# One matmul for all four groups of an involution's quarter, with its result picked out one row later

## The chip, the cores and the metric

The kernel runs on one core of one Trainium2 chip. The metric is the device time of one execution in microseconds. A core has a matrix engine (TensorE, in the profile PE for matmuls and PEld for weight loads), three engines for elementwise work (VectorE, DVE; ScalarE, ACT; GpSimd, POOL), a SyncE queue that issues most transfers (SP), and 16 DMA engines.

## The reference

Two residual layers work on x of shape 8 x 256 x 56 x 56 in float32. The change touches the first: an involution, a 7 x 7 convolution whose kernel differs from pixel to pixel and is shared by the 16 channels of a group.

```python
def _L0_conv_ref(x, w_reduce, b_reduce, w_span, b_span):   # K = 7, PAD = 3, G = 16
    ker = jnp.einsum('bchw,oc->bohw', x, w_reduce) + b_reduce[None, :, None, None]
    ker = jnp.einsum('bchw,oc->bohw', ker, w_span) + b_span[None, :, None, None]
    ker = ker.reshape(B, G, 1, K * K, H, W)
    xp = jnp.pad(x, ((0, 0), (0, 0), (PAD, PAD), (PAD, PAD)))
    patches = jnp.stack([xp[:, :, i:i + H, j:j + W] for i in range(K) for j in range(K)], axis=2)
    patches = patches.reshape(B, G, C // G, K * K, H, W)
    out = (ker * patches).sum(axis=3)
    return out.reshape(B, C, H, W)

x = x + _L0_conv_ref(_gn(x), ...)      # _gn: group norm, 32 groups
x = x + _L1_conv_ref(_gn(x), ...)      # two 3x3 ternary convolutions, batch norms, relu
```

## The kernel before, in words

The program has four stages, one after the other: the involution, the two convolutions of the second layer (`conv_phase`, matmuls at L385), and a last pass that adds everything up. The change is in the first stage.

**Tiles of the involution.** An image is cut into four quarters of 64 channels (four groups of 16 channels each, `GQ = 4`; `GP = 2` is the number of pairs of groups). The two halves of the picture's rows lie in one tile, the upper half on partitions 0 to 63 and the lower on 64 to 127. The picture is cut into small tiles of 3 x 8 pixels (`PY`, `PX`; `NP = 24`), seven across (`TX = 7`) and ten down each half (`TY = 10`; the tenth row of tiles is only one pixel high, so it has 8 pixels a tile). A small tile's outputs depend on 9 x 14 = 126 input pixels (`NQ`). So the involution of one small tile is a matmul: 126 input pixels are the contraction, the channels are the output rows, and the columns are output pixels.

**Generating the matrices.** `generate` makes, for the next quarter, the matrices `a` of 126 x (pixels) for each small tile and each group. It is cut into 14 units a quarter (`UNITS`): matmuls into a buffer `pg` of the ring `ps_p` (L629), then the bias is added on the way out, by ScalarE for some columns (L633) and by VectorE for the rest (L638), in that order. It yields after each unit. The loop takes two units in the even rows 0 to 8, one in the odd rows 1 to 7 and none in row 9 (`PER_ROW`). For the last quarter of an image `generate` also runs `reduce` for the next image (matmuls `pk`, L526, from the same ring, evacuated by ScalarE).

**Applying them.** `apply_row` does one row of small tiles of one quarter: for each of the seven tiles, each half of the picture and each pair of groups, one matmul of 32 channels by the columns of both groups of the pair, into the buffer `pa` of the ring `ps_a` (two buffers, L662). Each channel of a pair gets the result for its own group's matrix and for the other group's. `pick_out` takes what is wanted: ScalarE scales the even group's columns by 1 or 0 per partition (L674), VectorE adds the odd group's columns by 0 or 1 (L675), both into `inv` (three buffers), and GpSimd adds `inv` to x in place (L678).

**Input pixels.** They come from DRAM: `prep` normalizes a strip of x (GpSimd, `xn`, L559), transposes it (TensorE, `pt`, L567, also from `ps_p`), copies it to `stg` (ScalarE, L570) and stores it (`xtd`), three stores that `transfer` issues one a row. `load_q` brings the input pixels of a row of tiles, four rows ahead (`NQB`, L599).

**Order.** The loop runs over 32 quarters (8 images, four each) and over ten rows of tiles, 320 rows in all. In the order of the text, a row stores a part of the quarter before or loads a part of the next image (rows `X_AT`), issues one store of a strip, applies the row, prefetches, takes statistics for the norms on VectorE, picks out, generates for the next quarter, and does a step of a strip (rows `STRIP_AT`, counted over the 40 rows of an image). `pin()` holds each engine to that order. The core of it:

```python
row = apply_row(b, c, a, ty)
prefetch()
...
pick_out(b, c, ty, *row)
for _ in range(PER_ROW[ty]):
    next(gen, None)
if r in STRIP_AT:
    ...
    next(strips, None)
pin()
```

`ps_p` has three buffers of 1024 elements a partition, `ps_a` two of 512.

Of the kernel before, what the change touches and what calls it, by code (L numbers as in the profile page):

```python
# [7 lines left out]
F32 = mybir.dt.float32  # L8
F32R = mybir.dt.float32r
AF = mybir.ActivationFunctionType  # L10
ALU = mybir.AluOpType
AX = mybir.AxisListType
PSUM = bass.MemoryType.PSUM
DRAM = bass.MemoryType.DRAM

P = 128
# [10 lines left out]
CH = P // 2  # L27
NCQ = C // CH
GQ = G // NCQ
GP = GQ // 2  # L30
# [3 lines left out]
PY, PX = 3, 8  # L34
TY, TX = 10, W // PX
NP = PY * PX
# [3 lines left out]
NQ = QY * QX  # L40
# [34 lines left out]
@with_exitstack  # L75
def involution_tri_block_kernel(
    ctx: ExitStack, tc: tile.TileContext,
    x, w_red, b_red, w_line, b_tile, w1, w2, g1, b1, g2, b2, grp, ident, half, out,
):
    nc = tc.nc  # L80
    out = out.rearrange("b c h w -> b c (h w)")
# [53 lines left out]
    def image_stats(st, xt, j):  # L135
        nc.vector.bn_stats(st[:, j, :], xt[:, j * NC:(j + 1) * NC])  # L136
# [293 lines left out]


    with ExitStack() as ph1:
        ps_p = ph1.enter_context(tc.tile_pool(name="ps_p", bufs=3, space=PSUM))
        ps_a = ph1.enter_context(tc.tile_pool(name="ps_a", bufs=2, space=PSUM))

        def ps_tile(name):
# [7 lines left out]
        work = ph1.enter_context(tc.tile_pool(name="work", bufs=2))  # L444

        def load_x(b, c, j):

            if j == 0:
                xs[b, c] = xpool.tile([P, NHW], F32, tag="x", name=f"x_{b}_{c}")
            part = slice(j * NHW // 2, (j + 1) * NHW // 2)  # L450
            nc.sync.dma_start(xs[b, c][:, part], x[b, c, :, part])
# [35 lines left out]
        def fixed(shape, name, src=None):  # L487
            t_ = fix.tile(shape, F32, tag=name, name=name)
            if src is not None:
                nc.scalar.dma_start(t_, src)  # L490
            return t_

        ident_sb = fixed([P, P], "ident_sb", ident)
        half_sb = fixed([P, 2], "half_sb", half)
        wr, wrn = fixed([P, NCQ, CR], "wr"), fixed([P, NCQ, 2 * CR], "wrn")
        br, brn = fixed([P, 1], "br"), fixed([P, 1], "brn")
        for j in range(2):
# [90 lines left out]
        def transfer(n=1):  # L588
            while tasks and n:
                tasks.pop(0)()  # L590
                n -= 1
# [10 lines left out]
        def views(a):  # L602

            n = NT * GQ * NP
            return (a[:NQ, :n].rearrange("q (t f) -> q t f", t=NT),
                    a[:NQ, n:].rearrange("q (t f) -> q t f", t=NE))
# [41 lines left out]
        def apply_row(b, c, a, ty):  # L648


            ps = ps_a.tile([P, 512], F32, tag="pa", name=f"pa_{b}_{c}_{ty}")
            q = loads.pop((b, c, ty))
            whole, rest = views(a)
            if ty < TY - 1:
                av, n, t0, t1 = whole, NP, ty * TX, (TY - 1 + ty) * TX
            else:
                av, n, t0, t1 = rest, PX, 0, TX
            for k in range(TX):
                for h, t in enumerate((t0, t1)):
                    for g in range(GP):  # L660
                        o = h * CH + g * 32
                        nc.tensor.matmul(ps[o:o + 32, k * 2 * n:(k + 1) * 2 * n],  # L662
                                         q[:NQ, k, o:o + 32],
                                         av[:, t + k, g * 2 * n:(g + 1) * 2 * n],
                                         start=True, stop=True)
            return ps, n

        def pick_out(b, c, ty, ps, n):

            even, odd = (ps[:, :TX * 2 * n].rearrange("c (k h p) -> c k h p", k=TX, h=2)  # L670
                         [:, :, h] for h in range(2))
            inv = work.tile([P, TX, NP], F32, tag="inv", bufs=3, name=f"inv_{b}_{c}_{ty}")
            iv = inv[:, :, :n]
            nc.scalar.activation(iv, even, AF.Copy, scale=half_sb[:, 0:1])  # L674
            nc.vector.scalar_tensor_tensor(iv, odd, half_sb[:, 1:2], iv, ALU.mult, ALU.add)  # L675
            y, m = ty * PY, n // PX
            xv = xs[b, c][:, y * W:(y + m) * W].rearrange("p (y t x) -> p y t x", t=TX, x=PX)
            nc.gpsimd.tensor_tensor(  # L678
                xv, xv, iv.rearrange("p t (y x) -> p y t x", x=PX), ALU.add)

        queue = [(b, c, ty) for b in range(B) for c in range(NCQ) for ty in range(TY)]
        loads = {}
# [1 line left out]
        def prefetch():  # L684
            if queue:
                k = queue.pop(0)
                loads[k] = load_q(*k)

        def store_x1(b, c, h):
            nc.sync.dma_start(  # L690
                x1_d[b][c // 2][c % 2 * CH:(c % 2 + 1) * CH, h * NHW:(h + 1) * NHW],
                xs[b, c][h * CH:(h + 1) * CH])
# [3 lines left out]
        def gn2_stats(b, c, ty):  # L696

            if ty == 1:
                gst[b, c] = (small.tile([P, NCB, 6], F32, tag="gn_st2", name=f"st2_{b}_{c}"), 0)
            st, j = gst[b, c]  # L700
            while j < NCB and ((j + 1) * NC <= ty * PY * W or ty == TY):
                image_stats(st, xs[b, c], j)
                j += 1
            gst[b, c] = (st, j)
            if ty == TY:
                nc.vector.bn_aggr(mv2[:, b, c, :], st.rearrange("p n s -> p (n s)"))
# [4 lines left out]
        def pin(start=False):  # L711
            here = nc.cur_bb.bb.instructions
            fresh = []
            for i in reversed(here):
                if newest.get("all") is i:
                    break
                fresh.append(i)
            newest["all"] = here[-1]
            for i in reversed(fresh):
                if i.engine in newest and not start:  # L720
                    tc.add_manual_dep(
                        i, newest[i.engine].name,
                        mybir.DependencyInfo(mybir.DependencyClass.NoSync,
                                             mybir.DependencyReason.DATA),
                        reason="order of the text")
                newest[i.engine] = i
# [13 lines left out]
        def matrices(m):  # L740
            return (apool if m % 2 == 0 else apool1).tile(
                [P, (NT * NP + NE * PX) * GQ], F32, tag=f"a{m % 2}", name=f"a_{m}")
# [11 lines left out]
        quarters = [(b, c) for b in range(B) for c in range(NCQ)]  # L754


        X_AT = (0, 1, 4, 5, 6, 7, 8, 9)
        STRIP_AT = (23, 24, 26, 27, 29, 30, 32, 33, 35, 36, 38, 39, 2, 3, 5, 6)
        for _ in range(NQB):
            prefetch()  # L760
        pin(start=True)
        last = None
        strips = iter(())
        for m, (b, c) in enumerate(quarters):
            a = a_next
            gen = iter(())
            if m + 1 < len(quarters):
                a_next = matrices(m + 1)
                gen = generate(*quarters[m + 1], a_next)
            more = b + 1 < B  # L770
            for ty in range(TY):
                r = c * TY + ty

                if last is not None and ty in (2, 3):
                    store_x1(*last, ty - 2)
                elif more and r in X_AT:
                    load_x(b + 1, X_AT.index(r) // 2, X_AT.index(r) % 2)
                transfer()

                row = apply_row(b, c, a, ty)  # L780
                prefetch()

                if more and r >= 20:
                    if r == 20:
                        norm = params(b + 1)
                    next(norm, None)
                if ty == 1 and last is not None:
                    gn2_stats(*last, TY)
                elif ty >= 2:
                    gn2_stats(b, c, ty - 1)  # L790
                if more and 4 <= r < 20:
                    gn1_stats(b + 1, (r - 4) // NCB, (r - 4) % NCB)
                pick_out(b, c, ty, *row)
                for _ in range(PER_ROW[ty]):
                    next(gen, None)
                if r in STRIP_AT:
                    if r == STRIP_AT[0] and more:
                        strips = prep(b + 1)
                    next(strips, None)
                pin()  # L800
            for _ in gen:
                pass
            last = b, c
        gn2_stats(*last, TY)
        for h in range(2):
            store_x1(*last, h)
# [103 lines left out]
```

## Time and profile before

| what | value |
|---|---|
| time, median of 3 runs | 2447.73 us (2437.09 to 2450.58) |
| span of the profiled execution | 2443.3 us, mean granted clock 0.869 |
| TensorE busy, matmuls (PE) | 1780.2 us (73%), 30120 instructions |
| TensorE busy, weight loads (PEld) | 1670.4 us (68%), 30120 instructions |
| VectorE (DVE) | 1664.7 us (68%) |
| ScalarE (ACT) | 1125.6 us (46%) |
| GpSimd (POOL) | 286.8 us (12%) |
| L662 matmuls of apply_row | 17920, 289.8 us busy |
| L674, L675, L678 of pick_out | 320 each, 393, 368 and 518 ns on average |

Busy time is not the same as being the limit: matmuls overlap, so 17920 of them with 214 ns each take only 289.8 us together. A row of the chain of waits has a start in us, a length in us, and what the program's end hung on then. A row of the waits has us in total, times, and the longest in us. A row of the timeline has a start, a length, engine, line, operation and tiles, how many were merged (x), and in brackets the idle time before it and what ended it. "Issue" is time in which an engine waited for nothing that the profile shows.

### The profile page before, as it was taken

How to read it: one execution, taken by the hardware profiler on the slowest of the kernel's cores; microseconds unless marked ns; L12 is line 12 of the kernel's file. 1: busy time of each engine (PE TensorE's matmuls, PEld its weight loads, DVE VectorE, ACT ScalarE, POOL GpSimd, SP SyncE). 2: the span in 40 equal slices, each digit the busy share in tenths (PEclk: the TensorE clock that was granted, in tenths of full speed). 3: DMA queues.
4: the chain of work that ended last, by engine and by line, in shares of the span. 5: the costliest groups of instructions: out<-in, count | busy, mean ns of one | idle time of the engine just before them, and what ended most of it. 6: DMA issues, size and time to landing. Idle time of an engine off the chain costs nothing.

```text
span 2443.3 us, 68709 instructions
## 1 busy us (share of the span) xinstructions
PE 1780.2 (73%) x30120; PEld 1670.4 (68%) x30120; DVE 1664.7 (68%) x2554; ACT 1125.6 (46%) x2020; POOL 286.8 (12%) x427
## 2 busy tenths in 40 slices
PE   3407878788787877878767999999499999980000
PEld 2307767677676767767657999999499999980000
DVE  4566555564645556465548999999499999974444
ACT  1203434434343443434325666766456577654333
POOL 1101222222122231213210000000000000000000
PEclk8658989989898998999978999999699999995555
DMA  6627796978769597877765223322433233229998
GB/s 202 203 96 223 204 266 172 269 214 229 235 194 262 171 272 204 241 233 223 219 199 197 108 108 134 135 108 81 185 124 119 108 120 150 108 99 429 429 428 377
DMA packets 220294, 493.14 MB, mean 202 GB/s; under 512 B 38446, under 2 KB 139180, under 8 KB 211292
## 3 DMA queue, kind: packets, MB, share of 16 engines
q1 hardware_dynamic: 213680, 447.66, 55.9%
q10 hardware_dynamic: 6316, 41.09, 4.1%
q8 instruction: 237, 3.88, 0.6%
q14 instruction: 61, 0.50, 0.1%
HBM read 315.88 MB, written 172.81 MB: 200 GB/s over the span
## 4 chain that ended last, share of the span: by engine, by line
PE 65%; DMA 14%; issue 9%; DVE 7%; POOL 2%; ACT 1%; SPq 1%; ACTq 0%; POOLq 0%; DVEq 0%
PE c L385 35%; PE pg L629 15%; PE pa L662 9%; DMA y1f<-y1d 4%; DMA out_y<-x1f 3%; PE pt L567 3%; PE pk L526 3%; DVE a L638 2%; DMA q<-xtd 2%; POOL xn L559 1%; DVE x1f L848 1%; DMA x1f<-x1d 1%; DMA y1d<-y 1%; ACT a L633 1%; DMA wq<-wqd 1%
## 5 line engine op out<-in xcount | busy, mean ns | idle before, releaser
L385 PE MATMUL c<-pl,wq 128*128 128x392 f32 x4608 | 857.0, 348 | 52.1 <-ACT pl L291 32.7
L385 PEld LDWEIGHTS c<-pl,wq 128*128 128x128 f32 x4608 | 855.0, 189 | 53.8 <-ACT pl L291 33.4
L638 DVE TENSOR_TENSOR a<-pg,bt 126x756 f32<-126x756 f32 (+3 forms) x640 | 393.3, 657 | 278.0 <-ACT a L633 251.8
L629 PE MATMUL pg<-kr,wl 64*126 64x140 f32 (+1 forms) x6144 | 491.7, 308 | 62.6 <-issue 38.3
L629 PEld LDWEIGHTS pg<-kr,wl 64*126 64x126 f32 x6144 | 427.9, 209 | 87.8 <-issue 63.6
L662 PE MATMUL pa<-a,q 126*32 126x48 f32 x17920 | 289.8, 214 | 200.0 <-issue 123.7
L662 PEld LDWEIGHTS pa<-a,q 126*32 126x32 f32 x17920 | 237.4, 116 | 256.6 <-issue 202.6
L633 ACT ACTIVATE a<-pg,bt 126x126 f32<-126x126 f32 x768 | 244.2, 475 | 229.2 <-PE pg L629 228.9
L674 ACT ACTIVATE inv<-pa,half_sb 128x168 f32<-128x168 f32 x320 | 125.9, 393 | 405.6 <-PE pa L662 398.4
L678 POOL TENSOR_TENSOR x<-x,inv 128x168 f32<-128x168 f32 x320 | 165.8, 518 | 877.3 <-DVE inv L675 835.9
L675 DVE SCALAR_TENSOR_TENSOR inv<-pa,half_sb,inv 128x168 f32<-128x168 f32 x320 | 117.8, 368 | 211.6 <-ACT inv L674 211.4
L291 ACT CAST pl<-r 128x812 fp32r<-128x812 f32 x192 | 162.4, 867 | 152.3 <-DVE r L286 136.5
L348 ACT ACTIVATE dummy<-y,nc 128x1568 f32<-128x1568 f32 x128 | 205.4, 1605 | 15.6 <-DVE y L371 14.3
L292 DVE TENSOR_TENSOR pl<-r,pl 128x812 fp32r<-128x812 f32 x192 | 186.9, 1001 | 30.5 <-ACT pl L291 29.6
L136 DVE BATCH_NORM_STATS2 st<-x 128x6 f32<-128x392 f32 x256 | 138.2, 557 | 10.9 <-DMA x<-in_x 10.4
L829 ACT ACTIVATE xp<-raw,bi_bn,sc_bn 128x392 f32<-128x392 f32 (+1 forms) x128 | 84.8, 720 | 72.0 <-DVE a L286 57.1
L559 POOL TENSOR_SCALAR xn<-x,gn 128x784 f32<-128x784 f32 x64 | 108.3, 1692 | 55.9 <-DMA xtd<-xn 36.0
L819 ACT ACTIVATE xp<-raw,gn 128x392 f32<-128x392 f32 (+1 forms) x128 | 85.1, 721 | 57.0 <-DVE a L286 50.9
L567 PE MATMUL pt<-ident_sb,xn 128*112 128x128 f32 x512 | 81.6, 311 | 38.1 <-POOL xn L559 33.2
L570 ACT COPY stg<-pt 112x1024 f32<-112x1024 f32 x64 | 65.8, 1028 | 83.3 <-PE pt L567 53.2
L272 POOL MEMSET xp<- 128x116 f32 x32 | 6.3, 197 | 819.7 <-DVE a L286 819.5
L846 DVE SCALAR_TENSOR_TENSOR y1f<-y2f,sc_bn,y1f 128x3136 f32<-128x3136 f32 x16 | 55.8, 3485 | 64.8 <-DMA y2f<-y2d 64.8
(127 smaller groups left out, 1369.3 us busy)
## 6 DMA issues: line engine op xcount, KB each, us to landing
q<-xtd SPq DMA_DIRECT2D x320, 441.0 KB
xtd<-stg SPq DMA_DIRECT2D x64, 448.0 KB
raw<-x1d SPq DMA_DIRECT2D x32, 812.0 KB
raw<-y1d SPq DMA_DIRECT2D x32, 812.0 KB
x<-in_x SPq DMA_DIRECT2D x64, 392.0 KB
x1d<-x SPq DMA_DIRECT2D x64, 392.0 KB
y1d<-y SPq DMA_DIRECT2D x32, 784.0 KB
y2d<-y SPq DMA_DIRECT2D x32, 784.0 KB
```

The lines of the kernel that those rows point to most:

```text
L136: nc.vector.bn_stats(st[:, j, :], xt[:, j * NC:(j + 1) * NC])
L291: nc.scalar.copy(hi, r)
L292: nc.vector.tensor_tensor(lo, r, hi.bitcast(F32), ALU.subtract)
L348: nc.scalar.activation(dummy, y[:, to], f, bias=shift[:, to:to + 1], accum_out=stats[:, to, j, n:n + 1])
L385: nc.tensor.matmul(ps[:, to, :NM], wq[:, k, t, dx, to * P:(to + 1) * P], part[:, t, :, dx:dx + W], start=(c == 0), stop=(c == last))
L559: nc.gpsimd.tensor_scalar(xn[:, :, :, :TX].rearrange("p j r k -> p r k j"), xs[b, c][:, s * SR * W:(s + 1) * SR * W].rearrange("p (r k j) ...
L567: nc.tensor.transpose(pt[:NSP, j * P:(j + 1) * P], xn[:, j].rearrange("p r k -> p (r k)"), ident_sb)
L629: nc.tensor.matmul(dst, wl[rows, c, gp, o:o + NQ], kr[py][rows, px, :], start=True, stop=True)
L633: nc.scalar.activation(whole[:, g0 + i, p0 + j], ps[:NQ, i, j * nt:(j + 1) * nt], AF.Identity, bias=bt[:, c, g0 + i, p0 + j:p0 + j + 1])
L638: nc.vector.tensor_tensor(dst[:, g0:g0 + 2, p0:p0 + nv].rearrange("q g p t -> q g t p"), ps[:NQ, :, t0 * nv:t1 * nv].rearrange("q i (t p) ...
L662: nc.tensor.matmul(ps[o:o + 32, k * 2 * n:(k + 1) * 2 * n], q[:NQ, k, o:o + 32], av[:, t + k, g * 2 * n:(g + 1) * 2 * n], start=True, stop ...
L678: nc.gpsimd.tensor_tensor(xv, xv, iv.rearrange("p t (y x) -> p y t x", x=PX), ALU.add)
```

## The change

One matmul now does 64 channels by the columns of all four groups of a quarter, so a row of tiles has half as many. Each channel gets four results, of which one is its own group's. To pick it out there are twice as many scaled copies and fused adds as before, four a row, split between ScalarE and VectorE: three scaled copies and one fused add in even rows, two and two in odd rows, so that three or two partial sums are left, which GpSimd adds to x one by one. A row is picked out one row later, after the next row's matmuls are in the order. The buffer `pa` is twice as large, and the ring `ps_p` has two buffers in place of three. The loads of x come in every second row, a strip's steps every four rows in place of three, and the two stores of a quarter in rows 3 and 5 in place of 2 and 3.

```diff
-        ps_p = ph1.enter_context(tc.tile_pool(name="ps_p", bufs=3, space=PSUM))
+        ps_p = ph1.enter_context(tc.tile_pool(name="ps_p", bufs=2, space=PSUM))
...
-            ps = ps_a.tile([P, 512], F32, tag="pa", name=f"pa_{b}_{c}_{ty}")
+            ps = ps_a.tile([P, TX + 1, P], F32, tag="pa", name=f"pa_{b}_{c}_{ty}")
...
-                    for g in range(GP):
-                        o = h * CH + g * 32
-                        nc.tensor.matmul(ps[o:o + 32, k * 2 * n:(k + 1) * 2 * n],
-                                         q[:NQ, k, o:o + 32],
-                                         av[:, t + k, g * 2 * n:(g + 1) * 2 * n],
-                                         start=True, stop=True)
+                    nc.tensor.matmul(
+                        ps[h * CH:(h + 1) * CH, k, :GQ * n],
+                        q[:NQ, k, h * CH:(h + 1) * CH], av[:, t + k], start=True, stop=True)
...
-            inv = work.tile([P, TX, NP], F32, tag="inv", bufs=3, name=f"inv_{b}_{c}_{ty}")
-            iv = inv[:, :, :n]
-            nc.scalar.activation(iv, even, AF.Copy, scale=half_sb[:, 0:1])
-            nc.vector.scalar_tensor_tensor(iv, odd, half_sb[:, 1:2], iv, ALU.mult, ALU.add)
...
+            inv = work.tile([P, 3, TX, NP], F32, tag="inv", name=f"inv_{b}_{c}_{ty}")
...
+            iv = [inv[:, j, :, :n] for j in range(3)]
+            three = ty % 2 == 0
+            for j, g in enumerate((0, 1, 2) if three else (0, 1)):
+                nc.scalar.activation(iv[j], group(g), AF.Copy, scale=own_sb[:, g:g + 1])
+            for j, g in enumerate((3,) if three else (2, 3)):
+                nc.vector.scalar_tensor_tensor(iv[j], group(g), own_sb[:, g:g + 1], iv[j],
+                                               ALU.mult, ALU.add)
...
-            nc.gpsimd.tensor_tensor(
-                xv, xv, iv.rearrange("p t (y x) -> p y t x", x=PX), ALU.add)
+            for v in iv if three else iv[:2]:
+                nc.gpsimd.tensor_tensor(
+                    xv, xv, v.rearrange("p t (y x) -> p y t x", x=PX), ALU.add)
...
-        X_AT = (0, 1, 4, 5, 6, 7, 8, 9)
-        STRIP_AT = (23, 24, 26, 27, 29, 30, 32, 33, 35, 36, 38, 39, 2, 3, 5, 6)
+        X_AT = range(0, 16, 2)
+        STRIP_AT = (23, 24, 27, 28, 31, 32, 35, 36, 39, 0, 3, 4, 7, 8, 11, 12)
...
-                if last is not None and ty in (2, 3):
-                    store_x1(*last, ty - 2)
+                if last is not None and ty in (3, 5):
+                    store_x1(*last, (ty - 3) // 2)
...
-                row = apply_row(b, c, a, ty)
+                before, row = row, apply_row(b, c, a, ty)
...
-                pick_out(b, c, ty, *row)
+
+                if before is not None:
+                    pick_out(*before)
```

The statistics of the second norm move back by a row in the same way, and the last row is picked out after the loop.

More of the change, by code (lines that the diff above doesn't have):

```diff
@@ L77, in involution_tri_block_kernel @@
     ctx: ExitStack, tc: tile.TileContext,
-    x, w_red, b_red, w_line, b_tile, w1, w2, g1, b1, g2, b2, grp, ident, half, out,
+    x, w_red, b_red, w_line, b_tile, w1, w2, g1, b1, g2, b2, grp, ident, own, out,
 ):
@@ L493, in involution_tri_block_kernel @@
         ident_sb = fixed([P, P], "ident_sb", ident)
-        half_sb = fixed([P, 2], "half_sb", half)
+        own_sb = fixed([P, GQ], "own_sb", own)
         wr, wrn = fixed([P, NCQ, CR], "wr"), fixed([P, NCQ, 2 * CR], "wrn")
@@ L659, in apply_row, with group @@
                 for h, t in enumerate((t0, t1)):
-                    for g in range(GP):
-                        o = h * CH + g * 32
-                        nc.tensor.matmul(ps[o:o + 32, k * 2 * n:(k + 1) * 2 * n],
-                                         q[:NQ, k, o:o + 32],
-                                         av[:, t + k, g * 2 * n:(g + 1) * 2 * n],
-                                         start=True, stop=True)
-            return ps, n
-        def pick_out(b, c, ty, ps, n):
-            even, odd = (ps[:, :TX * 2 * n].rearrange("c (k h p) -> c k h p", k=TX, h=2)
-                         [:, :, h] for h in range(2))
-            inv = work.tile([P, TX, NP], F32, tag="inv", bufs=3, name=f"inv_{b}_{c}_{ty}")
-            iv = inv[:, :, :n]
-            nc.scalar.activation(iv, even, AF.Copy, scale=half_sb[:, 0:1])
-            nc.vector.scalar_tensor_tensor(iv, odd, half_sb[:, 1:2], iv, ALU.mult, ALU.add)
-            y, m = ty * PY, n // PX
+                    nc.tensor.matmul(
+                        ps[h * CH:(h + 1) * CH, k, :GQ * n],
+                        q[:NQ, k, h * CH:(h + 1) * CH], av[:, t + k], start=True, stop=True)
+            return b, c, ty, ps, n
+        def pick_out(b, c, ty, ps, n):
+            y, m = ty * PY, n // PX
+            inv = work.tile([P, 3, TX, NP], F32, tag="inv", name=f"inv_{b}_{c}_{ty}")
+            def group(g):
+                return ps[:, :TX, g * n:(g + 1) * n]
+            iv = [inv[:, j, :, :n] for j in range(3)]
[5 more added lines that the diff above has]
+                                               ALU.mult, ALU.add)
             xv = xs[b, c][:, y * W:(y + m) * W].rearrange("p (y t x) -> p y t x", t=TX, x=PX)
-            nc.gpsimd.tensor_tensor(
-                xv, xv, iv.rearrange("p t (y x) -> p y t x", x=PX), ALU.add)
+            for v in iv if three else iv[:2]:
+                nc.gpsimd.tensor_tensor(
+                    xv, xv, v.rearrange("p t (y x) -> p y t x", x=PX), ALU.add)
         queue = [(b, c, ty) for b in range(B) for c in range(NCQ) for ty in range(TY)]
@@ L761, in involution_tri_block_kernel @@
         pin(start=True)
-        last = None
+        last = row = None
         strips = iter(())
@@ L786, in involution_tri_block_kernel @@
                     next(norm, None)
-                if ty == 1 and last is not None:
+                if ty == 2 and last is not None:
                     gn2_stats(*last, TY)
-                elif ty >= 2:
-                    gn2_stats(b, c, ty - 1)
+                elif ty >= 3:
+                    gn2_stats(b, c, ty - 2)
                 if more and 4 <= r < 20:
                     gn1_stats(b + 1, (r - 4) // NCB, (r - 4) % NCB)
-                pick_out(b, c, ty, *row)
+                if before is not None:
+                    pick_out(*before)
                 for _ in range(PER_ROW[ty]):
@@ L803, in involution_tri_block_kernel @@
             last = b, c
+        pick_out(*row)
         gn2_stats(*last, TY)
@@ L875 @@
                     b_tile[px + kx, py + ky, :, :, py, px] = bs[:, :, ky, kx]
-    even = np.arange(P) // 16 % 2 == 0
     ins = {
@@ L895 @@
         "ident": np.eye(P, dtype=np.float32),
-        "half": np.stack([even, ~even], axis=1).astype(np.float32),
+        "own": np.repeat(np.tile(np.eye(GQ), (2, 1)), 16, axis=0).astype(np.float32),
     }
```

## The prediction

> **What bounds the kernel now.** I read the page's slices first (TensorE is busy in tenths 7 to 8, not 9, over the first half), then the chain of waits of the involution's row loop alone, then TensorE's own waits in it, then the timeline.
>
> The row loop runs from the first L662 matmul (183 us) to the last (1278 us): 1095 us, 320 rows, 3.42 us a row. The busy time of each engine in that stretch:
>
> ```profile
> core 0: us, PE busy (x) PEld busy (x) DVE busy (x) ACT busy (x) POOL busy (x), PEclk, DMA share, GB/s
> 183.00:1278.00 1095.00, 874.69 (x25132) 774.21 (x25130) 623.50 (x1359) 435.35 (x1176) 258.26 (x376) 0.91 0.77 223
> ```
>
> TensorE works 874.7 us of it, at a mean clock of 0.91; no other engine is near. What TensorE waits for there:
>
> ```profile
> PE pa L662 <- issue: 123.7, 70, 3.9
> PE pa L662 <- DMA q<-xtd: 58.8, 7, 52.4
> PE pg L629 <- issue: 38.3, 22, 4.6
> PE br L475 <- DVE gn L158: 12.7, 7, 2.0
> PE pa L662 <- DVE a L638: 11.9, 11, 1.4
> ```
>
> Of the 58.8 us, 52.4 is one wait before the loop. Real dependencies cost some 50 us in all; 164 us (123.7 + 38.3 + 2.3 at L567) is "issue", in 94 gaps. The timeline shows one:
>
> ```profile
> 617.37 0.62 PE L662 MATMUL pa<-a,q 126*32 126x48 f32 x37
> 620.24 0.69 PE L662 MATMUL pa<-a,q 126*32 126x48 f32 x19 [2.26 <-issue]
> ```
>
> 37 + 19 = 56 records are one row's matmuls, which wait for data only before the first: TensorE stood 2.26 us inside a row with nothing to wait for but its instructions. The DMA table names the source:
>
> ```profile
> q8 instruction: 237, 3.88, 0.6%
> ```
>
> 237 packets of 3.88 MB are 16.4 KB each; the program's 60,240 TensorE instructions (30120 loads, 30120 matmuls) at 64 B make 3.86 MB. So this queue is TensorE's instruction stream, and it shares DMA engines that are 77% busy. TensorE bounds the loop, by its stream of columns and by refills that come late.
>
> **What the skill says.** Runtime: NRT & Kernel Launch, Instruction fetch mechanics: instructions come in 16 KiB blocks of 256 over a DMA queue of the engine's own, and the cost of a boundary is mostly hidden. Size and queue agree with this trace; hidden it is not (94 gaps, 1.75 us on average). TensorEngine Tiling (Array Packing), Key Properties: tiles run their weight loads and matmuls in parallel. The trace agrees: below. TensorE: Matmul & The Clock Gate, Part 1: the clock falls to half after an idle window of about 3.4 us; the 0.91 above is such a mixture, so gaps also slow the work after them.
>
> **The change part by part.**
>
> *Wider matmuls (L662).* A row had 7 x 2 x 2 = 28 matmuls, 56 records (two passes), each 32 output channels and 48 columns; it gets 14 matmuls, 28 records, 64 channels and 96 columns. What a column costs, from the reduce matmuls and a row's matmuls:
>
> ```profile
> 551.97 3.40 PE pk L526 x32
> 576.16 0.73 PE pa L662 x56
> ```
>
> The 32 pk records are 16 of 280 and 16 of 224 columns on two row halves at once: 4032 columns in each half in 3.40 us, 0.84 ns a column. Then 48 columns take 40 ns; 56 records on four column groups at once are 14 rounds, 0.57 us, which with a tail of 0.16 us is the 0.73 us measured. So the old row already runs four matmuls side by side and is bound by its columns. The new one has two groups side by side: again 14 rounds, but of 96 columns, 81 ns: 1.13 + 0.16 + some 0.01 = 1.30 us. Plus 0.57 us on 288 full rows = +164 us, all on TensorE. The last rows of a quarter (32 columns for 16) stay near 0.6 us: their old records were issue-bound (112 in 1.28 us). Bounds: 1.15 us a row (+120) if loads overlap better than I think, 1.40 (+193) if worse.
>
> *Instructions.* 17,920 of the loop's 50,262 TensorE instructions go: 196 blocks become 126. Work per block was 874.7/196 = 4.5 us, and a late block cost 1.75 us more: a refill takes some 6 us, 9 at worst (gap of 4.6). Now a block holds (874.7 + 164 - 42)/126 = 7.9 us of work, so only the slowest refills, or blocks dense in instructions, still stall. I leave 22 of the 164 us: -142 us (bounds -100 and -160).
>
> *Clock.* At 0.91, 18% of the time was at half speed, which cost at most 0.09 x 875 = 79 us. With most gaps gone I take back half: -42 us (bounds -10 and -65).
>
> *New waits.* pick_out(r-1) now follows apply_row(r) and, on ScalarE and VectorE, the additions of row r-1's generation; the ps_a buffer of r-1 is needed by apply_row(r+1). How late that is:
>
> ```profile
> 645.62 2.03 PE L629 MATMUL pg<-kr,wl 64*126 64x126 f32 x32
> 646.81 1.76 ACT L633 ACTIVATE a<-pg,bt 126x126 f32<-126x126 f32 x6 [0.53 <-PE pg L629]
> 647.57 0.67 PEld L662 LDWEIGHTS pa<-a,q 126*32 126x32 f32 x56
> 648.11 1.53 DVE L638 TENSOR_TENSOR a<-pg,bt 126x504 f32<-126x504 f32 x2 [0.46 <-ACT a L633]
> 649.56 0.56 DVE L136 BATCH_NORM_STATS2 st<-x 128x6 f32<-128x392 f32 x1
> 650.04 0.37 DVE L675 SCALAR_TENSOR_TENSOR inv<-pa,half_sb,inv 128x168 f32<-128x168 f32 x1
> ```
>
> Two units leave TensorE at 647.57; their evacuation ends at 649.64, a statistic and the pick at 650.41: 2.84 us later. Meanwhile TensorE has one row with one unit: 1.30 + 0.97 = 2.27 us. It waits 0.5 us or so after each of the four two-unit rows of a quarter that a one-unit row follows, less where a strip's transposes (1.0 us) lie between, in two fifths of them: 1.2 us a quarter. The ps_p ring falls from three buffers to two (a ps_a tile grows from 512 to 1024 elements a partition). Strips now always transpose in rows with two units (rows 4, 8, 2, 6, 0 of a quarter; before, half of them did), so each finds the buffer of the unit before last still held: evacuated 1.5 to 2.1 us after that unit, covered by only 0.7 to 1.0 us of the next. Two strips a quarter, 1.1 us more than now. At a quarter's end row 9 has 0.6 us of work, and the next row 0 waits for the pick of row 8, 0.6 us later than for the additions it waits for now. Sum 2.9 us x 32 = 93 us; I take 82, since some fall on gaps that would be there (bounds 35 and 110). Queued behind the waiting matmuls is all TensorE work.
>
> *Evacuation.* A row has 2.5 scalings, 1.5 fused adds and 2.5 GpSimd adds for one of each. ScalarE +1.5 x (288 x 0.403 + 32 x 0.308) = +189, to 624 us; VectorE +59, to 683; GpSimd about +249, to 507. All lie beside TensorE in over 1095 us; I charge them only through the waits above. Moved x loads, stores and strips: no bytes change, and the load queue has room (it waits for TensorE itself): 0. The 1168 us outside the loop don't change.
>
> Sum: +164 - 142 - 42 + 82 = +62 us; 2447.7 + 62 = 2510 us.
>
> **The rivals.**
> *The refills win* (0.20). Waits stay at 20 because the delayed pick also takes ScalarE's waits for pa (398 us) out of the evacuation's way, the refills give 160 and the clock 55: 164 - 160 - 55 + 20 = -31, 2417 us. For it: the 164 us of "issue" are the largest idle item. Against it: VectorE at 683 us with fewer buffers behind a denser TensorE.
> *A wash* (0.10). Refills -155, clock -50, waits 45: +4, 2452 us.
> *The 64-wide groups don't overlap* (0.04). 14 rounds become 28: 28 x 81 = 2.27 + 0.16 us a row, +1.70 x 288 = +490, less 160 for refills and 65 for clock: 2713 us. Against it: four 32-wide groups overlap now.
> *DMA becomes the bound.* At a share of 0.77 it could do the loop in 843 us; no reason for it.
>
> **Numbers.** Forecast 2510 us (0.66 for slower by this mechanism, 0.70 with the serial case), faster 0.20, same 0.10. The range reaches down to the first rival, 2415, and up to where pa at 1.40 us (+29), refills at -100 (+42) and waits at 110 (+28) are mostly together: 2595.
>
> **What would show it.** Right: pa row at about 1.3 us on the chain; "issue" below 50 us in the loop; mean clock there about 0.95; new TensorE waits at pa and pt for VectorE and ScalarE of 80 to 150 us in all. Wrong: a pa row under 1.0 us, "issue" still above 100 us, or pa and pt waits no more than now.

## The result, and the profile after

The changed kernel takes 2566.3 us (median), 1.051 times the time of before (95% interval 1.0468 to 1.0551; the quotient of the two medians, 1.049, lies within it). The forecast was 2510 us, slower, in a range of 2415 to 2595: right in direction and range, about half the size. All of the difference lies in the row loop, which now runs from 183 to 1399 us, 1216 us in place of 1095.

The busy time of each engine in that stretch (the same view as before):

```profile
core 0: us, PE busy (x) PEld busy (x) DVE busy (x) ACT busy (x) POOL busy (x), PEclk, DMA share, GB/s
183.00:1399.00 1216.00, 1013.34 (x16168) 899.58 (x16164) 663.87 (x1517) 542.06 (x1656) 502.88 (x854) 0.94 0.69 200
```

TensorE is busy 139 us longer, at a mean clock of 0.94, and idle 203 us, against 220 before. So its idle time hardly changed in sum. Its make-up did; TensorE's waits in the loop (us in total, times, longest):

```profile
PE pa L661 <- DVE inv L679: 61.7, 76, 1.5
PE pa L661 <- issue: 38.0, 17, 2.6
PE pt L567 <- DVE a L638: 28.3, 27, 1.3
PE pg L629 <- DVE a L638: 23.5, 14, 2.1
PE pt L567 <- POOL x L683: 19.1, 15, 1.3
PE br L475 <- DVE gn L158: 10.3, 7, 1.5
PE pk L526 <- DVE a L638: 8.2, 7, 1.2
```

"Issue" fell from 164 us to 38 while the instruction queue went from 237 blocks to 167:

```profile
q8 instruction: 167, 2.74, 0.4%
```

Even those 38 us are not refills. Before the change, 91 of the loop's 93 "issue" gaps lay among the matmuls of one row or of its units; now all 17 stand between the last row of a quarter and row 0 of the next, and in all 17 TensorE goes on 0.10 us after a pick ends on VectorE. The timeline at one of them (row 9's short matmuls, then row 0 of the next):

```profile
562.16 1.01 PE L661 MATMUL pa<-a,q 126*64 126x32 f32 x28
562.69 1.53 DVE L638 TENSOR_TENSOR a<-pg,bt 126x504 f32<-126x504 f32 x2 [1.88 <-ACT a L633]
...
564.14 1.02 DVE L136 BATCH_NORM_STATS2 st<-x 128x6 f32<-128x392 f32 x2
565.20 0.27 DVE L461 BATCH_NORM_AGGREGATE mv<-st 128x2 f32<-128x24 f32 x1
565.38 0.69 DVE L679 SCALAR_TENSOR_TENSOR inv<-pa,own_sb,inv 128x168 f32<-128x168 f32 x3
565.77 2.24 PEld L661 LDWEIGHTS pa<-a,q 126*64 126x64 f32 x28 [2.72 <-issue]
...
565.80 2.51 PE L661 MATMUL pa<-a,q 126*64 126x96 f32 x28 [2.63 <-issue]
```

TensorE stands 2.63 us, and starts 0.10 us after the first of VectorE's three fused adds ends (at 565.70): it waited for the pick of row 8, though the profile names no releaser. On VectorE that pick stood behind the additions of row 8's units, two statistics and an aggregation. The row that follows then takes 2.51 us in place of 1.38, 1.1 us more, because the clock has gone to half, and it stays there for 10 us (columns as above; the clock is the 0.50):

```profile
565.80:575.70 9.90, 8.60 (x82) 7.79 (x82) 3.21 (x10) 0.98 (x3) 2.24 (x6) 0.50 0.27 81
```

TensorE: Matmul & The Clock Gate, Part 1, of the Trainium skill says that TensorE goes to half its clock after at least one idle window of about 3.4 us; here 2.63 idle us were enough.

The row itself is as forecast. TensorE's matmuls of one row and the units after it:

```profile
589.72 1.38 PE L661 MATMUL pa<-a,q 126*64 126x96 f32 x28
...
591.02 1.66 PEld L629 LDWEIGHTS pg<-kr,wl 64*126 64x126 f32 x28
```

591.02 - 589.72 = 1.30 us, against 0.73 before.

### The profile page after: what moved, and what is told of

Read it like the earlier page. It is cut to its first block, busy times and chain, and to the rows that moved or that the text cites. A ratio compares the mean times of both kernels' runs of the same rounds, so it can differ in the third digit from the quotient of the medians.

```text
span 2563.9 us, 52574 instructions
## 1 busy us (share of the span) xinstructions
PE 1922.6 (75%) x21160; PEld 1799.2 (70%) x21160; DVE 1706.0 (67%) x2714; ACT 1232.6 (48%) x2500; POOL 532.0 (21%) x907
## 4 chain that ended last, share of the span: by engine, by line
PE 38%; DMA 10%; issue 3%; DVE 2%; POOL 2%; ACT 1%; SPq 0%; POOLq 0%; ACTq 0%; DVEq 0%
PE c L385 33%; DMA y1f<-y1d 4%; DMA out_y<-x1f 3%; PE pa L661 2%; PE pg L629 1%; POOL x L683 1%; DVE x1f L856 1%; DMA y2f<-y2d 1%; DMA y1d<-y 1%; DMA wq<-wqd 1%; DMA q<-xtd 0%; PE pk L526 0%; DVE a L638 0%; DMA xtd<-stg 0%; PE pt L567 0%
## 5 line engine op out<-in xcount | busy, mean ns | idle before, releaser
L661 PE MATMUL pa<-a,q 126*64 126x96 f32 x8960 | 459.2, 257 | 151.8 <-DVE inv L679 61.7
L683 POOL TENSOR_TENSOR x<-x,inv 128x168 f32<-128x168 f32 (+1 forms) x800 | 414.8, 521 | 754.5 <-DVE inv L679 716.1
L661 PEld LDWEIGHTS pa<-a,q 126*64 126x64 f32 x8960 | 400.2, 144 | 202.9 <-issue 99.2
L629 PE MATMUL pg<-kr,wl 64*126 64x140 f32 (+1 forms) x6144 | 462.6, 297 | 56.6 <-DVE a L638 56.2
L629 PEld LDWEIGHTS pg<-kr,wl 64*126 64x126 f32 x6144 | 400.8, 199 | 95.0 <-issue 35.3
L677 ACT ACTIVATE inv<-pa,own_sb 128x168 f32<-128x168 f32 (+1 forms) x800 | 256.4, 405 | 173.1 <-PE pa L661 131.2
L679 DVE SCALAR_TENSOR_TENSOR inv<-pa,own_sb,inv 128x168 f32<-128x168 f32 (+1 forms) x480 | 158.9, 362 | 158.2 <-ACT inv L677 142.7
L570 ACT COPY stg<-pt 112x1024 f32<-112x1024 f32 x64 | 64.8, 1013 | 145.5 <-PE pt L567 145.5
L567 PE MATMUL pt<-ident_sb,xn 128*112 128x128 f32 x512 | 74.4, 292 | 77.1 <-POOL xn L559 29.7
L567 PEld LDWEIGHTS pt<-ident_sb,xn 128*112 128x112 f32 x512 | 58.8, 142 | 90.5 <-POOL x L683 49.2
```

What stands on the lines that cost most here:

```text
L629: nc.tensor.matmul(dst, wl[rows, c, gp, o:o + NQ], kr[py][rows, px, :], start=True, stop=True)
L661: nc.tensor.matmul(ps[h * CH:(h + 1) * CH, k, :GQ * n], q[:NQ, k, h * CH:(h + 1) * CH], av[:, t + k], start=True, stop=True)
L677: nc.scalar.activation(iv[j], group(g), AF.Copy, scale=own_sb[:, g:g + 1])
L679: nc.vector.scalar_tensor_tensor(iv[j], group(g), own_sb[:, g:g + 1], iv[j], ALU.mult, ALU.add)
L683: nc.gpsimd.tensor_tensor(xv, xv, v.rearrange("p t (y x) -> p y t x", x=PX), ALU.add)
```

## The experiments

Times are medians; ratios are to the kernel before, run on the same chip (2438 to 2442 us there).

**The pick at once again, in the changed kernel.**

```diff
-                before, row = row, apply_row(b, c, a, ty)
+                row = apply_row(b, c, a, ty)
...
-                if before is not None:
-                    pick_out(*before)
+                pick_out(*row)
```

> The changed kernel (2566 us) with each row picked out at once again, statistics back by a row, all else as changed. Theory A (column stream of the wide matmuls, less refills, plus waits that the late pick and the two-buffer ring make): the waits of TensorE's pa matmuls for the VectorE pick (62 us in the row loop) go, 50 to 80 us faster, 2485 to 2515 us. Rival B (what costs is the larger amount of evacuation on ScalarE, VectorE and GpSimd): as many operations as before, and ScalarE waits for pa again, so 2550 to 2590 us.

Measured: 2458.1 us, ratio 1.007 (1.0043 to 1.0097): 108 us faster than the changed kernel, more than theory A asked for. The loop, and TensorE's waits in it (the three largest, and the one at pa for the pick):

```profile
183.00:1291.00 1108.00, 975.03 (x16159) 869.05 (x16155) 666.82 (x1515) 585.40 (x1656) 506.22 (x853) 0.98 0.75 219
```

```profile
PE pt L567 <- DVE a L638: 45.5, 42, 1.3
PE pg L629 <- DVE a L638: 30.1, 27, 2.1
PE pa L661 <- DVE a L638: 15.4, 14, 1.1
...
PE pa L661 <- DVE inv L679: 0.5, 1, 0.5
```

Idle time falls from 203 to 133 us, busy time from 1013 to 975, as the clock goes from 0.94 to 0.98. The evacuation is as large as in the changed kernel (VectorE 667 us, GpSimd 506 us). No "issue" row is left with the same 42,320 TensorE instructions. So one row's delay of the pick cost 108 us: 70 of waiting and 38 of slower clock. At pa itself 99 us of waits go (the 61.7 for the pick and the 38.0 of "issue"); about 30 come back elsewhere, half of them at pa for VectorE's additions.

**As many instructions as before, the same columns.**

```diff
-                for h, t in enumerate((t0, t1)):
-                    nc.tensor.matmul(
-                        ps[h * CH:(h + 1) * CH, k, :GQ * n],
...
+                for s in range(2):
+                    for h, t in enumerate((t0, t1)):
+                        nc.tensor.matmul(
+                            ps[h * CH:(h + 1) * CH, k, s * 2 * n:(s + 1) * 2 * n],
...
```

> The changed kernel with each 96-column matmul cut in two of 48 columns: the same columns, the same evacuation, but 56 records a row again, so TensorE's instructions come back to 60,240. Theory A: the refills are late again, issue in the row loop goes from 38 us to 90 to 150 us, and the time rises by 50 to 110 us, 2615 to 2675 us. Rival C (the issue gaps of before had another cause than the number of instructions): within 15 us of 2566.

Measured: 2653.2 us, ratio 1.087 (1.0823 to 1.0913). The time lies where theory A put it, but not for its reason: "issue" is 35 us. What grew is the row itself; the last line is the last row of a quarter, with 16 columns:

```profile
610.46 1.84 PE L662 MATMUL pa<-a,q 126*64 126x48 f32 x56
612.23 1.86 PE L629 MATMUL pg<-kr,wl 64*126 64x126 f32 x28
...
215.19 1.81 PE L662 MATMUL pa<-a,q 126*64 126x16 f32 x56
```

1.77 us for 56 records, 32 ns each, where the columns would need 1.13 + 0.16; a third of the columns takes as long. A pair of a 64-wide load and its matmul has a floor of some 32 ns here (the 32-wide pairs of before ran at 13). On refills the run tells little. Of its 35 us of "issue", 23 stand at quarter ends and end 0.10 us after a pick, as in the changed kernel; 12 us in 16 gaps lie among the matmuls of a row or its units, where the changed kernel has none:

```profile
198.68 0.72 PE L662 MATMUL pa<-a,q 126*64 126x48 f32 x17 [0.47 <-issue]
```

So some late refills came back with the instructions, but few. That a block of 256 instructions lasts longer at this pace (about 1146 us / 196 = 5.8 us of work, an estimate, against 4.5 before) would explain why; it is not shown.

**Half of the columns.** Leaves out the products of two of the four groups.

```diff
-                        ps[h * CH:(h + 1) * CH, k, :GQ * n],
-                        q[:NQ, k, h * CH:(h + 1) * CH], av[:, t + k], start=True, stop=True)
+                        ps[h * CH:(h + 1) * CH, k, :2 * n],
+                        q[:NQ, k, h * CH:(h + 1) * CH], av[:, t + k, :2 * n], start=True, stop=True)
...
```

> The changed kernel with the products of two of the four groups left out: 64 channels by 48 columns, the picks read the two groups that are there twice over. Instructions, evacuation and waits in the order are those of the changed kernel, only the column stream is halved. Theory A: a row takes 0.73 us in place of 1.30, 164 us less work; since some of it turns into waits for evacuation, 90 to 150 us faster, 2415 to 2475 us. Rival B: evacuation sets the pace, within 25 us of 2566.

Measured: 2550.9 us, ratio 1.045 (1.0413 to 1.0479), only 15 us faster than the changed kernel. Theory A missed. Part is the floor just named; a row with 48 columns takes

```profile
594.68 1.02 PE L661 MATMUL pa<-a,q 126*64 126x48 f32 x28
...
595.63 0.96 PEld L629 LDWEIGHTS pg<-kr,wl 64*126 64x126 f32 x16
```

0.95 us, so the saving is (1.30 - 0.95) x 288 = 101 us, not 164. The rest came back: the waits at pa for the pick rose from 61.7 to 91.7 us, and the clock over the loop fell to 0.88:

```profile
183.00:1383.00 1200.00, 969.19 (x16172) 866.16 (x16172) 661.44 (x1515) 541.56 (x1655) 500.65 (x852) 0.88 0.70 203
```

Idle time rose from 203 to 231 us, and busy time fell by 44 us only, so some 57 of the 101 us went into the slower clock. In the changed kernel, then, a shorter stream of columns gains little: the chain from a row's units over their evacuation to the pick and back to pa sets the pace, and the gaps that it makes bring the clock down.

**Two of four picks.** Leaves out two groups' scaled copies and adds: one scaled copy, one fused add, one GpSimd add.

```diff
-            for j, g in enumerate((0, 1, 2) if three else (0, 1)):
+            for j, g in enumerate((0,)):
...
-            for j, g in enumerate((3,) if three else (2, 3)):
+            for j, g in enumerate((1,)):
...
-            for v in iv if three else iv[:2]:
+            for v in iv[:1]:
```

> The changed kernel with the picks of two of the four groups left out: one scaled copy, one fused add, one GpSimd add a row, as before the change; matmuls and order as changed. Theory A: the pick's chain gets 0.4 to 1.2 us shorter, which takes part of the waits at pa and pt, 20 to 60 us faster, 2505 to 2545 us. Rival B: nearly all of the loss goes, 2440 to 2480 us.

Measured: 2537.0 us, ratio 1.039 (1.0355 to 1.0421), 29 us faster. The doubled evacuation is worth 29 us beside a late pick, the lateness 108.

**The late pick alone, in the kernel before.** The edit of the first experiment the other way round.

> The kernel before with nothing changed but that each row is picked out one row later (the second norm's statistics move back with it). Theory A2 (the late pick stands behind the evacuation of the units of its own row, so that the pa buffer of a row is free only after the next row's matmuls are long done): TensorE gets waits for VectorE's pick at pa of 50 to 120 us, some of them in place of late refills, and the time rises by 40 to 110 us, 2480 to 2550 us. Rival D (the late pick costs only with the two-buffer ring and the larger evacuation of the changed kernel): within 15 us of before, 2427 to 2457 us.

Measured: 2494.3 us, ratio 1.023 (1.0179 to 1.0277). With 32-wide matmuls, half the evacuation and three buffers in `ps_p`, a late pick alone costs 2.3%. Rival D falls. TensorE's waits named for the pick are only 19.0 us, and "issue" is 191 us in place of 164:

```profile
PE pa L662 <- issue: 146.7, 89, 3.3
PE pg L629 <- issue: 40.8, 26, 3.9
PE pa L662 <- DVE inv L675: 19.0, 33, 2.3
```

But 30 of these "issue" gaps, 58 us, stand before the first matmul of a row, where before had none at pa, and end 0.05 to 0.10 us after a pick:

```profile
247.08 1.35 PE L662 MATMUL pa<-a,q 126*32 126x48 f32 x56 [2.60 <-issue]
```

So the late pick costs 77 us of waits at pa, in part in place of late refills, which fall from 164 to 133 us.

**Two buffers in ps_p alone, in the kernel before.**

```diff
-        ps_p = ph1.enter_context(tc.tile_pool(name="ps_p", bufs=3, space=PSUM))
+        ps_p = ph1.enter_context(tc.tile_pool(name="ps_p", bufs=2, space=PSUM))
```

> The kernel before with two buffers in the ring ps_p in place of three, nothing else. Theory A3: transposes and units wait for VectorE's additions, 60 to 110 us of waits, part of them in place of late refills, 20 to 60 us slower, 2460 to 2500 us. Rival: the ring isn't short in this order, within 12 us of 2440.

Measured: 2513.2 us, ratio 1.031 (1.0283 to 1.0341): 75 us, above what was expected. The waits that came:

```profile
PE pg L629 <- DVE a L638: 45.5, 67, 2.1
...
PE pt L567 <- DVE a L638: 14.2, 21, 1.2
```

**The late pick with room for it.** As the last kernel, with the late pick and four buffers in `ps_a`.

```diff
-        ps_a = ph1.enter_context(tc.tile_pool(name="ps_a", bufs=2, space=PSUM))
+        ps_a = ph1.enter_context(tc.tile_pool(name="ps_a", bufs=4, space=PSUM))
```

> The kernel before with the pick one row later, four pa buffers in place of two, and two buffers in the ring ps_p to make room. Theory A3 (a late pick costs only because a pa buffer isn't free in time): its waits at pa for the pick are gone, and it runs within 15 us of the kernel before with two buffers in ps_p. Rival H (a late pick delays the evacuation of the units on ScalarE and VectorE too): 30 us or more slower than that.

Measured: 2506.7 us, ratio 1.029 (1.0264 to 1.0319), the same as the one before it without the late pick (1.0283 to 1.0341). No wait at pa for the pick is left among its waits, and one gap of 0.2 us is all the "issue" before a row. So the late pick adds nothing here once pa has four buffers: what it costs otherwise is the missing buffer, and rival H falls. The same kernel with a late pick, two pa buffers and the ring of two was not run. So it is the waits at pa, not the time alone, that speak against a cost hidden behind the ring's own waits.

**The new places alone, in the kernel before.** `X_AT`, `STRIP_AT` and the stores as in the change.

> The kernel before with only the new places of the x loads, the strips' steps and the two stores. Theory A2: with three buffers in the ring the transposes find one free, and the same bytes move, so within 15 us of before. Rival E (the new places even out the load on the DMA engines, so that refills come sooner): issue in the row loop falls by 30 us or more and the time by 25 to 60 us.

Measured: 2457.7 us, ratio 1.0088 (1.0042 to 1.0135), a little slower, just outside the 15 us; "issue" is 159 us. Rival E falls: the new places don't bring the refills sooner.

**Half of the loads of input pixels, in the kernel before.** Leaves out the loads of odd rows, which use the even rows' tile.

```diff
...
-                loads[k] = load_q(*k)
+                if k[2] % 2 == 0:
+                    newest_q["q"] = load_q(*k)
+                loads[k] = newest_q["q"]
```

> The kernel before with the loads of the odd rows' input pixels left out (an odd row uses the tile of the even row before it), everything else the same: half of the 141 MB of those loads go. Theory A2 (refills of the instruction stream come late because they share busy DMA engines): issue in the row loop falls from 164 us below 80 and the time by 70 to 140 us, 2305 to 2375 us. Rival G (a block's refill has a fixed length whatever else moves): issue stays above 140 us, and the time falls by at most 20 us.

Measured: 2380.4 us, ratio 0.975 (0.9708 to 0.9782), 58 us faster, between the two. The loop's share of the DMA engines falls from 0.77 to 0.59, and the waits for "issue" from 164 to 112 us:

```profile
PE pa L662 <- issue: 69.7, 51, 3.0
PE pg L629 <- issue: 40.3, 26, 3.4
```

So other transfers do delay the refills. How much of the 112 us that are left is the doing of the other half is not shown: the DMA engines are still 59% busy.

**Transposes in rows with one unit.** The pick at once, and

```diff
-        STRIP_AT = (23, 24, 27, 28, 31, 32, 35, 36, 39, 0, 3, 4, 7, 8, 11, 12)
+        STRIP_AT = (22, 23, 26, 27, 30, 31, 34, 35, 38, 39, 2, 3, 6, 7, 10, 11)
```

> The changed kernel with the pick at once (2458 us) and the strips' transposes moved to rows with one unit or none (22, 23, 26, 27, and so on: a row earlier or later). Theory A2: the transposes then find a buffer of the two-buffer ring evacuated; their 45 us of waits for VectorE's additions go below 15, 25 to 50 us faster, 2408 to 2433 us, below the kernel before. Rival F (the wait moves on to the next user of the ring): within 12 us of 2458.

Measured: 2457.4 us, ratio 1.0068 (1.0044 to 1.0093), no change from 2458. The ring's wait at pt is gone, and another has taken its place:

```profile
PE pt L567 <- POOL xn L559: 47.8, 36, 2.2
```

The strip is normalized on GpSimd in the row before, an even row with three adds ahead of it, and isn't ready. Rival F was right that the wait moves, but not where to.

**And normalized three rows ahead.**

```diff
+        STRIP_AT = (22, 25, 26, 29, 30, 33, 34, 37, 38, 1, 2, 5, 6, 9, 10, 13)
```

> The changed kernel with the pick at once, transposes in rows with one unit or none, and each strip's normalization three rows ahead of its transposes in place of one. Theory A3 (the transposes wait for whatever comes last of two things, a buffer of the two-buffer ring and the strip that GpSimd normalizes behind its additions): both are there, the waits at pt go from 49 and 57 us below 15, 25 to 50 us faster than 2458, 2408 to 2433 us, faster than before the change. Rival F (the wait moves on to the next user of the ring or to pa): within 12 us of 2458.

Measured: 2429.9 us, ratio 0.9971 (0.9957 to 0.9984), 24 to 28 us (by the ratios or the medians) faster than with the pick at once alone, and a little faster than before the change. The loop ends at 1260 us:

```profile
183.00:1259.90 1076.90, 985.32 (x16166) 878.66 (x16163) 666.87 (x1515) 581.96 (x1654) 505.07 (x851) 0.96 0.77 226
```

```profile
PE pg L629 <- DVE a L638: 27.3, 21, 2.1
...
PE pt L567 <- DVE a L638: 3.5, 14, 0.3
```

**Those places in the kernel before.**

> The kernel before (32-wide matmuls, pick at once, three buffers in ps_p) with the places of loads, stores and strips of the run that was 0.3% faster than before. Theory A3 (these places help only with a ring of two; with three the transposes found a buffer anyway, and refills stay late): within 20 us of the kernel before, 2420 to 2460 us, so the gain of that run is the wide matmul's. Rival: the places alone make before faster by 25 us or more, below 2415 us.

Measured: 2437.2 us, ratio 1.0007 (0.9985 to 1.003). The places alone bring nothing, so the 0.3% belong to the wide matmul with places that suit it. They are small; the two intervals (0.9957 to 0.9984 and 0.9985 to 1.003) barely miss each other.

## Why the prediction was right, and where it was too small

*What bounds it* was right for before: TensorE, with refills late (93 gaps by the lines shown, not 94). It no longer held after the change, where halving the columns gained 15 us and moving the pick 108.

*Wider matmuls, +164.* Right for the full rows: 1.30 us measured, 0.57 more than before. The last rows of a quarter, which I left as they were, went from some 0.55 us to some 0.90 (28 records at the 32 ns floor): 32 x 0.35, an estimate of +11 us, that I missed. The 112 records in 1.28 us that I took for last rows are one last row and the full row after it.

*Instructions, -142.* A little small: none of the changed kernel's "issue" gaps is a refill, and with the pick at once no "issue" is left, so the term was -164. The cause was in part shown: fewer instructions and no such gaps go together, splitting the matmuls brought 12 us of them back, and taking other traffic away shortened them; a run with only the number of instructions changed doesn't exist here, as the split run changed the row's length too.

*Clock, -42.* Too large. By difference it gave about -36 (busy time +139 = 164 + 11 - 36); priced as I had priced it, (1 - 0.91) x 875 = 79 us before and (1 - 0.94) x 1013 = 61 after, it gave -18. With the pick at once the mean clock reaches 0.98, so it was the late pick's gaps that kept it at 0.94.

*New waits, +82.* The term that was mis-sized. Waits other than refills rose from 56 us (220 - 164) to 203, so +147, beyond my bound of 110. Pa after the pick, pt for the ring and the quarter's end were where I had put them; pg for the ring (23.5 us) and pt for GpSimd's additions (19.1 us) I had not named. Both parts were too small. I had charged the late pick with 1.2 + 0.6 us a quarter, 58 us of the 93 in all; undoing it gave 70 us of waits and, by the clock that its gaps cost, another 38. I had priced each wait and the clock as if one didn't make the other. The ring I had at 1.1 us a quarter, 35 us, for the transposes alone; the other 77 of the 147 stay with the pick at once, where pt and pg wait 75.6 us for VectorE's additions. In the kernel before, the third buffer is worth 75 us too. The two parts don't simply add up in time: pick at once with two buffers is only 16 us above before.

Sum of the terms: +164 + 11 - 36 - 164 + 147 = +122, against 1216 - 1095 = 121. As clock and waits were taken by difference, this must come out; it is a split, not a test.

The range held in part by luck: the waits passed their bound, and the room that the range had kept for slow refills and a row of 1.40 us took it up.

*Evacuation, 0 beyond the waits.* 29 us by the run with two picks, within the waits already counted. The busy times forecast came close for VectorE (683 us, measured 664) and GpSimd (507 and 503), too high for ScalarE (624 and 542). Outside the loop are 1348 us, not 1168, in both kernels; nothing hangs on it. *Moved places, 0.* +0.9% in the kernel before, and with a ring of two they matter by 28 us.

*The rivals.* "The refills win" had the size of the refills right (-160) and said what would have to hold: waits that stay at 20. With the pick at once and strips placed for the ring, that is nearly what happened. The 64-wide groups do overlap: 1.30 us, not 2.43.

## What to carry to other kernels

An operation moved one step later in every queue holds its input buffer over everything that now stands ahead of it; count buffers for the whole of that time before moving it, and don't pay for it with another ring's buffer. Where the clock falls after a gap, as it did here after 2.63 us, price a new gap with the slower work behind it. Where a wait has no named releaser, look at where it stands: inside a row of matmuls it was the instruction stream here, before a row's first it was a buffer. When instructions can be halved by doing more columns in each, look for the gaps that the instruction stream causes, and set them against the added columns one to one: here +175 and -164.

## What the runs showed of the hardware

Pairs of a 126 x 64 float32 weight load and its matmul don't follow each other faster than about 32 ns (56 in 1.81 us with 16 columns, 56 in 1.77 us and 28 in 0.95 us with 48), while 126 x 32 pairs of 48 columns run at 13 ns (56 in 0.73 us). With 16 to 48 columns a 64-wide matmul was bound by that; with 96 it took 46 ns a pair (28 in 1.30 us).
